# Seven PSUM banks as one ring of score tiles in a fused four-layer graph network

## The chip, the cores and the metric

The kernel runs on one core of a Trainium2 chip. The time is the device time of one execution in microseconds (us), given as the median of several runs. A separate execution is recorded by the hardware profiler; its own time stands beside its span below. TensorE, ScalarE, VectorE, GpSimd and SyncE appear as PE, ACT, DVE, POOL and SP, as in the profile; PEld is PE's weight load.

## The reference, cut to what matters

Four residual layers work on x (3327 x 128) with one dense matrix adj (3327 x 3327). Nearly all of the time goes into layer 0, an attention with 128 heads (the reference reshapes q, k and v so that the 128 features are the heads and 8 is the width of each), adj being added twice to the scores:

```python
h = jnp.maximum(_layernorm(x, axis=-1), 0.0)
q = (h @ Wq.T).reshape(d, n, 8)          # d = 128 heads, n = 3327
k = (h @ Wk.T).reshape(d, n, 8)
v = (h @ Wv.T).reshape(d, n, 8)
a = jnp.einsum('dnh,dmh->dnm', q, k) * d ** -0.5 + adj + adj
a = jax.nn.softmax(a, axis=2)
out = jnp.einsum('dnm,dmh->dnh', a, v).reshape(n, 8 * d)
x = x + out @ Wo.T
```

Three more layers follow, each built of layer norms, 128 x 128 projections and one or two products with adj. The change does not touch them.

## The kernel before, in words

**Stages.** First q, k and v are projected, split and written to DRAM, together with a bound for each row's scores (0 to about 457 us of the span). Then comes the attention (457 to 10552 us). The other three layers take the rest. Only the attention's loop is changed.

**Tiling.** Scores are held transposed: 128 keys on the partitions, up to 476 queries (a column, c, of 7; the last has 472) along the free axis. Heads go four at a time (a group, g, of 32), and the 26 key tiles two at a time (q, of 13). One (c, g, q) is a *pair* u: an even and an odd key tile of the same four heads. There are 7 x 32 x 13 = 2912 pairs. A pair needs two PSUM banks, one for each tile, of 2 KB per partition.

**What happens to a pair.** `seed` (L632, DVE) copies adj minus the row bound into the two banks. For head j = 0 `scores` (L638, PE) adds q times k onto the seed, one matmul for each tile, even (r = 0) first; the two use the upper and the lower 64 rows of the array. `exps` (L650, ACT) reads both banks in one instruction (128 x 952) and writes exp to an SBUF tile `e`. For j = 1 to 3 PE adds, onto the same banks, the next head's product together with the negated product of the last head, so that the bank again holds the scores of one head, and ACT takes the next exp. After the fourth exp (j = 3) the banks are free. `values` (L658, PE) multiplies the four `e` tiles by v, the four heads side by side in four column groups of the array, into one further bank `po`; each call is eight matmuls on PE. After 13 pairs `po` holds a group's result, and `store` (L670, DVE) copies it to `OS`, from which POOL issues four DMAs (L674). The next group's first `values` must wait for that copy, since there is one `po`.

**The order of the work** is written out by hand as a loop over slots i, one exp in each; each engine follows it in order. Slot 4m is the first exp (j = 0) of pair m, slot 4m+1 the last (j = 3) of pair m-2, slot 4m+2 the third (j = 2) of pair m-1, slot 4m+3 the second (j = 1) of pair m. So a pair's exps stand at slots 4m, 4m+3, 4m+6 and 4m+9. In every odd slot PE gets a *block*: the scores for the next two slots, then one `values` call. In slot 4m+1 that is the scores of slots 4m+2 and 4m+3 and `values` of pair m-3's odd tile; in slot 4m+3 the scores of slots 4m+4 (pair m+1, j = 0) and 4m+5, and `values` of pair m-2's even tile. The store of pair m-3, if it is the last of its group, stands in slot 4m+2. Now and then slot 4m+3 has other DVE work (`Square`: transposes and a reduction of adj, L283 and L287, about 1 us each).

**The banks before.** Seven banks are for scores, in three PSUM tiles of 3, 2 and 2 banks; pair u uses tile u % 3. With the 3-bank tile, pairs alternate between banks (0, 1) and (2, 1): the even tile's seed goes to a free bank in slot 4m, the odd tile's, in slot 4m+2, waits for the last exp of the pair three before. With a 2-bank tile both seeds stand in slot 4m+1 behind that last exp, which is issued in two halves of 128 x 476, so that the even seed can start after the first half. A one-element memset `apart` (L742) stands between the two seeds. So 1941 of the 2912 pairs have their j = 3 exp in halves.

**Dependencies.** `touch` tells the framework for each instruction that touches score banks which earlier ones it needs not wait for (other banks of the tile, on another engine; with the 2-bank tiles on DVE too), and adds a dependency on the last one that touched the same bank.

Of the kernel before, what the change touches and what calls it, by code (L numbers as in the profile page):

```python
# [9 lines left out]

DVE = mybir.EngineType.DVE
F32 = mybir.dt.float32


# [3 lines left out]
AF = mybir.ActivationFunctionType  # L18
# [5 lines left out]
P = 128  # L24
# [49 lines left out]
def width_of(c):  # L74

    return min(CW, N + 1 - c * CW)
# [8 lines left out]
def gnn_kernel(ctx: ExitStack, tc: tile.TileContext, x, adj, Wq, Wk, Wv, Wo, embed, layer,  # L85
               embed_bias, layer_bias, weight, bias, W_in, W_out, out):
    nc = tc.nc
# [171 lines left out]
    class Square:  # L259
# [29 lines left out]
        def store(self):  # L289
            nc.sync.dma_start(by_tile[:, :, self.s * P:(self.s + 1) * P].rearrange("t p n -> p t n"), self.cols)  # L290
# [144 lines left out]
    with tc.tile_pool(name="d1", bufs=1) as d1, tc.tile_pool(name="d2", bufs=2) as d2, \  # L435
# [17 lines left out]
        with tc.If(loose > 0):  # L453
            for s in range(squares_of(0), NT):
                square(d2, s, d2)
            for t in range(NT):
# [5 lines left out]
                with tc.For_i(0, HEADS, 1) as d:  # L462
# [3 lines left out]
                    for r in range(2):  # L466
                        for b in range(4):
# [4 lines left out]
                                             start=True, stop=True)  # L472
# [9 lines left out]
            for c in range(NC):  # L482
                c0 = c * CW
                w = min(CW, N - c0)
# [3 lines left out]
                with tc.For_i(0, HEADS, 1) as d:  # L488
# [11 lines left out]
                    po = d_ps.tile([P, CW], F32, name="po_x")  # L500
                    for t in range(NT):
                        m = rows_of(t)
                        s = d_ps.tile([P, 4 * P], F32, name="ps_y")
# [6 lines left out]
                                         start=(t == 0), stop=(t == NT - 1))  # L510
# [9 lines left out]
    with tc.tile_pool(name="e1", bufs=1) as e1, tc.tile_pool(name="e_adj", bufs=30) as e_adj, \  # L520
# [7 lines left out]
        VA = [e1.tile([P, NT, 4, H + 1], F32, name=f"VA{i}") for i in range(2)]  # L528

        seen = e1.tile([P, 3], F32, name="seen")  # L530
        apart = e1.tile([1, 1], F32, name="apart")
        S = [e_ps.tile([P, 3 if i == 0 else 2, 512], F32, name=f"S{i}") for i in range(3)]
        po = e_ps.tile([P, 512], F32, name="po")

        def load_qk(c, g):
# [53 lines left out]
        with tc.If(loose < 1), tc.manual_schedule():  # L589
# [4 lines left out]
            for i in range(2):  # L594
                nc.vector.memset(QS[i][:, 0, :].bitcast(F32), 0.0)

            for bank in [s[:, i, :] for s in S for i in range(s.shape[1])] + [po]:
                nc.tensor.matmul(bank[:, :CW], zero[:, :P], zero, start=True, stop=True)

            pairs = [(c, g, q) for c in range(NC) for g in range(NG) for q in range(NQ)]  # L600
            n = len(pairs)
            adj_of, shift_of, v_of, e_of, here = {}, {}, {}, {}, {}

            def banks(u):


                return [2 * (u // 3 % 2), 1] if u % 3 == 0 else [0, 1]

            touched = [deque(maxlen=12) for i in range(3)]
            last = {}
            after = mybir.DependencyInfo(mybir.DependencyClass.Sync, mybir.DependencyReason.DATA)

            def touch(u, rows, x):
                of = {banks(u)[r] for r in rows}
                for y, other in touched[u % 3]:
                    if not of & other and (x.ins.engine != y.ins.engine or u % 3 and x.ins.engine == DVE):
                        tc.declare_no_dep(x.ins, y.ins, reason="other banks")
                for i in of:  # L620
                    if (u % 3, i) in last:
                        tc.add_manual_dep(x.ins, last[u % 3, i].ins.name, after, reason="the same bank")
                    last[u % 3, i] = x
                touched[u % 3].append((x, of))

            def bank(u, r):
                return S[u % 3][:, banks(u)[r], :width_of(pairs[u][0])]

            def seed(u, r):
                c, g, q = pairs[u]  # L630
                w = width_of(c)
                touch(u, [r], nc.vector.tensor_copy(bank(u, r), adj_of[c][2 * q + r][:, :w]))  # L632

            def scores(u, j):
                c, g, q = pairs[u]
                w, b = width_of(c), (c * NG + g) % 2
                for r in range(2):
                    x = nc.tensor.matmul(  # L638
                        bank(u, r), KT[b][64 * r:64 * r + 64, max(0, j - 1), q * P:(q + 1) * P],
                        QS[b][64 * r:64 * r + 64, j, :w], start=False, stop=True, skip_group_check=True)  # L640
                    if (j, q, r) == (0, 0, 0):
                        tc.add_manual_dep(x.ins, here.pop(c * NG + g).ins.name, after, reason="the loads")
                    touch(u, [r], x)

            def exps(u, j):
                w, lo = width_of(pairs[u][0]), min(banks(u))
                e = e_of[u, j] = e_e.tile([P, 2, CW], F32, name=f"e{j}", bufs=(5, 4, 3, 2)[j])

                for a, b in ((0, 2),) if j < 3 or u % 3 == 0 else ((0, 1), (1, 2)):
                    touch(u, range(a, b), nc.scalar.activation(e[:, a:b, :w], S[u % 3][:, lo + a:lo + b, :w],  # L650
                                                               AF.Exp, scale=2.0))

            def values(u, r):
                c, g, q = pairs[u]
                w, k = width_of(c), c * NG + g
                at = banks(u)[r] - min(banks(u))
                for j in range(4):
                    nc.tensor.matmul(po[32 * j:32 * j + H + 1, :w], VA[k % 2][:, 2 * q + r, j, :],  # L658
                                     e_of[u, j][:, at, :w], start=(q == 0 and r == 0),
                                     stop=(q == NQ - 1 and r == 1))  # L660
                if r == 0:
                    return
                for j in range(4):
                    del e_of[u, j]
# [11 lines left out]
            def loads(u):  # L676

                c, g, q = pairs[u]
                k = c * NG + g
                if k + 1 < NC * NG:  # L680
                    nxt = divmod(k + 1, NG)
                    if q == 1:
                        load_qk(*nxt)
                        v_of[k + 1] = load_v(*nxt)
                    if q == 4:
                        negate_q(*nxt)
                        spread_v(*nxt, v_of.pop(k + 1))
                        here[k + 1] = all_here(*nxt)
                if c + 1 < NC and (g, q) == (0, 0):
                    plan_squares(c)  # L690
                if g == NG - 1 and c + 1 < NC:
                    if q == 0:
                        shift_of[c + 1] = load_shift(c + 1)
                        adj_of[c + 1] = []
                    while len(adj_of[c + 1]) < min(NT, 2 * q + 6):
                        adj_of[c + 1].append(load_adj(c + 1, len(adj_of[c + 1]), shift_of[c + 1]))
# [29 lines left out]
            def in_slot(i):  # L726

                j = -i % 4
                return (i - 3 * j) // 4, j


            for i in range(-4, 4 * n + 15):
                u, j = in_slot(i)
                if 0 <= u < n:
                    exps(u, j)

                u, at = (i + 4) // 4, i % 4
                if u < n and (u % 3 == 0 and at in (0, 2) or u % 3 and at == 1):
                    for r in range(2) if at == 1 else (at // 2,):
                        seed(u, r)  # L740
                        if at == 1 and r == 0:
                            nc.vector.memset(apart, 0.0)  # L742
                u = (i - 14) // 4
                if at == 2 and 0 <= u < n and pairs[u][2] == NQ - 1:
                    store(u)
                if at == 3 and i > 0:
                    for f, a in behind.pop(i // 4, ()):
                        f(*a)
                if at % 2:
                    for k in (1, 2):  # L750
                        u, j = in_slot(i + k)
                        if 0 <= u < n:
                            scores(u, j)
                    u, r = ((i - 11) // 4, 0) if at == 3 else ((i - 13) // 4, 1)
                    if 0 <= u < n:
                        values(u, r)
                if at == 0 and 0 <= i // 4 < n:
                    loads(i // 4)
# [110 lines left out]
    def arr(name, w=D):  # L869
        return big.tile([P, NT, w], F32, name=name)  # L870
# [121 lines left out]
    with tc.tile_pool(name="g1", bufs=1) as g1:  # L992
# [6 lines left out]
        a, aa = arr("a", D + 1), sm.new()  # L999
# [12 lines left out]
        f = sm.div(sm.artanh(yn, L1_MAX_TANH), yn)  # L1012
        al, be = sm.mul(al, f), sm.mul(be, f)
        y = arr("y")
# [31 lines left out]
    with tc.tile_pool(name="h1", bufs=1) as h1:  # L1046
# [4 lines left out]
        a, aa = arr("a", D + 1), sm.new()  # L1051
# [9 lines left out]
        f = sm.mul(sm.div(sm.artanh(pn, L2_MAX_TANH), pn), pf)  # L1061
        al, be = sm.mul(al, f), sm.mul(be, f)
        y = arr("y")
# [6 lines left out]
        u, rr = arr("y"), sm.new()  # L1070
# [88 lines left out]
```

## Time and profile before

| what | value |
|---|---|
| median of 3 runs | 11516.81 us (11514.25 to 11517.72) |
| the profiled execution's own time | 11513.99 us |
| its span | 11512.2 us |
| mean granted PE clock over the span; in 457 to 10552 us | 0.978; 1.00 |
| stage 457 to 10552 us | 10095 us |
| exps, L650 | 13589 instructions |
| seeds, L632 | 5824 instructions, mean 660 ns |
| scores, L638 | 23296 matmuls |
| values, L658 | 46592 matmuls |
| copies of `po`, L670 | 224 instructions, 653 ns |
| `apart`, L742 | 1941 instructions, 59 ns |

A line of the costliest groups reads: source line, engine, operation, output<-input, shapes, count | busy time in us, mean ns of one | idle time of the engine before them and who ended it. The duration of one instruction starts when it is issued to its engine; where the one before is still running, the two overlap, so that a mean duration can be longer than the step from one to the next. A line of the timeline reads: start in us, length in us, engine, line, operation and count (neighbours of a kind are merged), and in brackets the engine's idle time before it and who ended it.

### The profile page before, as it was taken

To read this page: it belongs to the slowest core of one execution; us is meant where nothing else is said; L and a number is where in the kernel's file an instruction comes from. 1 tells how busy PE (TensorE), PEld (TensorE's weight loads), DVE (VectorE), ACT (ScalarE), POOL (GpSimd) and SP (SyncE) were. 2 spreads that over 40 slices of the span, in tenths; PEclk is the share of its full clock that TensorE was granted. 3 is DMA by queue.
4 is the path that set the end of the run, shared out by engine and by line. 5 is a ranking of instruction groups with operands and counts; after the bars stand their busy time and mean duration, and the time that the engine had idled before them with its cause. 6 is when DMAs were issued, how large, how long until landed. Compare 5 with 4: busy or idle time off the path is not lost.

```text
span 11512.2 us, 196520 instructions
## 1 busy us (share of the span) xinstructions
PE 11042.9 (96%) x72980; PEld 3752.1 (33%) x72980; DVE 4640.8 (40%) x9456; ACT 10396.0 (90%) x14091; POOL 1895.0 (16%) x3261
## 2 busy tenths in 40 slices
PE   4599999999999999999999999999999999998879
PEld 2233333333333333333333333333333333333544
DVE  5344443444434343343443444434443333334633
ACT  3599999999999999999999999999999999997220
POOL 5211112111121111211112111121111211111000
PEclk7799999999999999999999999999999999999889
DMA  8755555555455554555555545555554544444447
GB/s 248 248 88 94 90 89 109 87 92 92 87 109 89 90 93 75 108 90 90 93 88 107 92 88 93 90 106 93 87 92 80 100 83 77 84 78 111 163 173 272
DMA packets 652613, 1242.80 MB, mean 108 GB/s; under 512 B 185966, under 2 KB 527990, under 8 KB 635148
## 3 DMA queue, kind: packets, MB, share of 16 engines
q1 hardware_dynamic: 609768, 1100.61, 49.0%
q0 software_dynamic: 41888, 129.51, 3.7%
q8 instruction: 590, 9.67, 0.4%
q14 instruction: 367, 3.01, 0.1%
HBM read 1082.90 MB, written 146.60 MB: 107 GB/s over the span
## 4 chain that ended last, share of the span: by engine, by line
ACT 59%; PE 31%; issue 4%; DVE 1%; DMA 0%; POOL 0%; SPq 0%; POOLq 0%; DVEq 0%; ACTq 0%
ACT e L650 59%; PE po L658 13%; PE S L638 12%; PE pu L952 5%; PE pu L904 0%; PE ps_y L848 0%; PE pu L927 0%; DVE OS L670 0%; DVE xs L939 0%; DMA ot<-oT_d 0%; PE pu L915 0%; DVE s L955 0%; DMA KT<-kS_d 0%; PE ps_t L844 0%; DVE s L935 0%
## 5 line engine op out<-in xcount | busy, mean ns | idle before, releaser
L650 ACT ACTIVATE e<-S 128x952 f32<-128x952 f32 (+3 forms) x13589 | 10091.6, 1067 | 4.0 <-PE S L638 3.7
L632 DVE COPY S<-a 128x476 f32<-128x476 f32 (+1 forms) x5824 | 3620.0, 660 | 6100.6 <-ACT e L650 6052.3
L658 PE MATMUL po<-e,VA 128*9 128x476 f32 (+1 forms) x46592 | 5737.2, 564 | 15.7 <-DVE OS L670 4.3
L638 PE MATMUL S<-QS,KT 64*128 64x476 f32 (+1 forms) x23296 | 5147.0, 446 | 24.9 <-DVE S L632 20.2
L638 PEld LDWEIGHTS S<-QS,KT 64*128 64x128 f32 x23296 | 2530.0, 183 | 5254.9 <-ACT e L650 2390.7
L674 POOL DMA_DIRECT2D oT_d<-OS x896 | 470.8, 531 | 5563.0 <-DVE OS L670 5455.6
L658 PEld LDWEIGHTS po<-e,VA 128*9 128x9 f32 x46592 | 691.6, 88 | 1644.7 <-issue 1545.0
L559 POOL TENSOR_SCALAR QS<-QS 32x476 fp32r<-32x476 f32 (+1 forms) x1344 | 781.9, 582 | 1345.7 <-DMA QS<-qS_d 772.7
L124 ACT COPY uT<-pu 128x494 f32<-128x494 f32 (+1 forms) x12 | 6.6, 546 | 426.9 <-PE pu L952 426.9
L569 POOL COPY VA<-VR 128x832 f32<-128x832 f32 x224 | 198.3, 885 | 977.2 <-DMA VR<-v_d 767.7
L952 PE MATMUL pu<-strip,h 128*128 128x494 f32 (+2 forms) x728 | 293.8, 564 | 38.9 <-ACT h L885 38.9
L952 PE MATMUL pu<-strip,y 128*128 128x494 f32 (+2 forms) x728 | 295.1, 568 | 29.2 <-DVE y L939 18.2
L580 POOL TENSOR_TENSOR a<-a,shb 128x476 f32<-128x476 f32 (+1 forms) x182 | 213.2, 1206 | 242.6 <-DMA a<-adjT 219.7
L283 DVE STREAM_TRANSPOSE cols<-rows 128x416 f32<-128x416 f32 x208 | 199.6, 964 | 21.8 <-DMA rows<-in_adj_dram 13.8
L952 PEld LDWEIGHTS pu<-strip,h 128*128 128x128 f32 (+1 forms) x728 | 138.1, 191 | 190.8 <-issue 141.4
L952 PEld LDWEIGHTS pu<-strip,y 128*128 128x128 f32 (+1 forms) x728 | 139.4, 192 | 184.1 <-issue 153.2
L670 DVE COPY OS<-po 128x476 f32<-128x476 f32 (+1 forms) x224 | 146.2, 653 | 40.9 <-PE po L658 34.1
L124 ACT COPY hT<-pu 128x494 f32<-128x494 f32 (+1 forms) x4 | 2.2, 546 | 136.2 <-PE pu L952 136.2
L415 ACT CAST st_k<-st_q 128x1664 fp32r<-128x1664 f32 x16 | 53.7, 3377 | 75.4 <-DMA st_q<-kraw_d 57.9
L955 DVE TENSOR_REDUCE s<-strip 128x1 f32<-128x3327 f32 (+1 forms) x26 | 93.9, 3616 | 61.6 <-DMA strip<-in_adj_dram 61.6
L950 POOL DMA_DIRECT2D strip<-adjT x39 | 20.8, 532 | 589.1 <-PE pu L952 576.5
L340 PE MATMUL ps_t<-wk,hT 128*128 128x512 f32 x104 | 58.8, 700 | 60.8 <-ACT sq L362 60.8
(178 smaller groups left out, 1840.1 us busy)
## 6 DMA issues: line engine op xcount, KB each, us to landing
KT<-kS_d SPq DMA_DIRECT2D x1792, 208.0 KB
KT<-kS_d SPq DMA_DIRECT2D x1792, 104.0 KB
VR<-v_d SPq DMA_DIRECT2D x224, 416.0 KB
strip<-adjT POOLq DMA_DIRECT2D x39, 1663.5 KB, 7.1
strip<-adjT SPq DMA_DIRECT2D x36, 1663.5 KB
QS<-qS_d SPq DMA_DIRECT2D x3072, 14.9 KB
QS<-qS_d SPq DMA_DIRECT2D x1536, 29.8 KB
adjT<-cols SPq DMA_DIRECT2D x26, 1664.0 KB
```

The costliest lines, as they stand in the source:

```text
L283: nc.vector.transpose(self.cols[:, t0:t0 + NQ, 32 * j:32 * j + 32], self.rows.rearrange("p (x t) -> p t x", t=NT)[:, t0:t0 + NQ, :])
L559: nc.gpsimd.tensor_scalar(QS[b][r0:r0 + 32, j + 1, :w], QS[b][r0:r0 + 32, j, :w].bitcast(F32), -1.0, 0.0, op0=ALU.mult, op1=ALU.add)
L569: nc.gpsimd.tensor_copy(VA[(c * NG + g) % 2][:, :, :, 0:H], v.rearrange("p j (t e) -> p t j e", e=H))
L580: nc.gpsimd.tensor_tensor(a[:, :w], a[:, :w], shift[:, :w], op=ALU.subtract)
L632: touch(u, [r], nc.vector.tensor_copy(bank(u, r), adj_of[c][2 * q + r][:, :w]))
L638: x = nc.tensor.matmul(bank(u, r), KT[b][64 * r:64 * r + 64, max(0, j - 1), q * P:(q + 1) * P], QS[b][64 * r:64 * r + 64, j, :w], start=Fa ...
L650: touch(u, range(a, b), nc.scalar.activation(e[:, a:b, :w], S[u % 3][:, lo + a:lo + b, :w], AF.Exp, scale=2.0))
L658: nc.tensor.matmul(po[32 * j:32 * j + H + 1, :w], VA[k % 2][:, 2 * q + r, j, :], e_of[u, j][:, at, :w], start=(q == 0 and r == 0), stop=(q ...
L670: nc.vector.tensor_copy(o[:, :w], po[:, :w])
L674: nc.gpsimd.dma_start(oT_d[:, d * N + c * CW:d * N + c * CW + w], o[32 * j:32 * j + H + 1, :w])
L952: nc.tensor.matmul(pu[c][:, :w], y[:m, t, :], s[:m, c * AW:c * AW + w], start=(t == 0), stop=(t == NT - 1))
L955: nc.vector.tensor_reduce(deg[:m, t:t + 1], s[:m], axis=AX.X, op=ALU.add)
```

## The change

The three score tiles become one tile of seven banks, a ring. Pair u takes the banks `odd = (4 - 2u) % 7` and `even = odd + 1` (modulo 7): (even, odd) is (5, 4), (3, 2), (1, 0), (6, 5), (4, 3), (2, 1), (0, 6), and then the same again. So the even bank of pair u becomes the odd bank of pair u+3, and its odd bank the even bank of pair u+4. Both seeds stand in slot 4m+1: first the odd one of pair m+1, then the even one of pair m+2, both behind the last exp of pair m-2. Only where u % 7 is 6 do the two banks not lie side by side; there each of the four exps is issued in two halves, even first. All other exps are whole. In `e` the odd tile comes first now. `apart` is gone. `touch` keeps one list of the last 48 accesses, and no longer frees a DVE instruction from waiting for another DVE instruction.

```diff
-        S = [e_ps.tile([P, 3 if i == 0 else 2, 512], F32, name=f"S{i}") for i in range(3)]
+        S = e_ps.tile([P, 7, 512], F32, name="S")
...
             def banks(u):
-                return [2 * (u // 3 % 2), 1] if u % 3 == 0 else [0, 1]
-            touched = [deque(maxlen=12) for i in range(3)]
+                odd = (4 - 2 * u) % 7
+                return (odd + 1) % 7, odd
+            touched = deque(maxlen=48)
...
-                for y, other in touched[u % 3]:
-                    if not of & other and (x.ins.engine != y.ins.engine or u % 3 and x.ins.engine == DVE):
+                for y, other in touched:
+                    if not of & other and x.ins.engine != y.ins.engine:
                         tc.declare_no_dep(x.ins, y.ins, reason="other banks")
...
             def exps(u, j):
-                w, lo = width_of(pairs[u][0]), min(banks(u))
+                w, (even, odd) = width_of(pairs[u][0]), banks(u)
                 e = e_of[u, j] = e_e.tile([P, 2, CW], F32, name=f"e{j}", bufs=(5, 4, 3, 2)[j])
-                for a, b in ((0, 2),) if j < 3 or u % 3 == 0 else ((0, 1), (1, 2)):
-                    touch(u, range(a, b), nc.scalar.activation(e[:, a:b, :w], S[u % 3][:, lo + a:lo + b, :w],
-                                                               AF.Exp, scale=2.0))
+                if even > odd:
+                    touch(u, (0, 1), nc.scalar.activation(e[:, :, :w], S[:, odd:even + 1, :w], AF.Exp, scale=2.0))
+                    return
+                for r in range(2):
+                    touch(u, [r], nc.scalar.activation(e[:, 1 - r, :w], bank(u, r), AF.Exp, scale=2.0))
...
-                u, at = (i + 4) // 4, i % 4
-                if u < n and (u % 3 == 0 and at in (0, 2) or u % 3 and at == 1):
-                    for r in range(2) if at == 1 else (at // 2,):
-                        seed(u, r)
-                        if at == 1 and r == 0:
-                            nc.vector.memset(apart, 0.0)
+                at = i % 4
+                if i == -4:
+                    seed(0, 0)
+                if at == 1:
+                    for u, r in (((i + 3) // 4, 1), ((i + 7) // 4, 0)):
+                        if u < n:
+                            seed(u, r)
```

More of the change, by code (lines that the diff above doesn't have):

```diff
@@ L9 @@
 from concourse.masks import make_identity
-DVE = mybir.EngineType.DVE
 F32 = mybir.dt.float32
@@ L530, in gnn_kernel @@
         seen = e1.tile([P, 3], F32, name="seen")
-        apart = e1.tile([1, 1], F32, name="apart")
-        S = [e_ps.tile([P, 3 if i == 0 else 2, 512], F32, name=f"S{i}") for i in range(3)]
+        S = e_ps.tile([P, 7, 512], F32, name="S")
         po = e_ps.tile([P, 512], F32, name="po")
@@ L595, in gnn_kernel @@
                 nc.vector.memset(QS[i][:, 0, :].bitcast(F32), 0.0)
-            for bank in [s[:, i, :] for s in S for i in range(s.shape[1])] + [po]:
+            for bank in [S[:, i, :] for i in range(7)] + [po]:
                 nc.tensor.matmul(bank[:, :CW], zero[:, :P], zero, start=True, stop=True)
@@ L616, in touch @@
                 of = {banks(u)[r] for r in rows}
-                for y, other in touched[u % 3]:
-                    if not of & other and (x.ins.engine != y.ins.engine or u % 3 and x.ins.engine == DVE):
+                for y, other in touched:
+                    if not of & other and x.ins.engine != y.ins.engine:
                         tc.declare_no_dep(x.ins, y.ins, reason="other banks")
                 for i in of:
[L621 to L624, printed above, removed]
+                    if i in last:
+                        tc.add_manual_dep(x.ins, last[i].ins.name, after, reason="the same bank")
+                    last[i] = x
+                touched.append((x, of))
             def bank(u, r):
-                return S[u % 3][:, banks(u)[r], :width_of(pairs[u][0])]
+                return S[:, banks(u)[r], :width_of(pairs[u][0])]
             def seed(u, r):
@@ L655, in values @@
                 w, k = width_of(c), c * NG + g
-                at = banks(u)[r] - min(banks(u))
                 for j in range(4):
                     nc.tensor.matmul(po[32 * j:32 * j + H + 1, :w], VA[k % 2][:, 2 * q + r, j, :],
-                                     e_of[u, j][:, at, :w], start=(q == 0 and r == 0),
+                                     e_of[u, j][:, 1 - r, :w], start=(q == 0 and r == 0),
                                      stop=(q == NQ - 1 and r == 1))
```

## The prediction, written before the changed kernel ran

> **What bounds the kernel now.** I read the page's busy times first, then the costliest groups, then the stage's busy time.
>
> ```profile
> PE 11042.9 (96%) x72980; PEld 3752.1 (33%) x72980; DVE 4640.8 (40%) x9456; ACT 10396.0 (90%) x14091; POOL 1895.0 (16%) x3261
> ...
> L650 ACT ACTIVATE e<-S 128x952 f32<-128x952 f32 (+3 forms) x13589 | 10091.6, 1067 | 4.0 <-PE S L638 3.7
> L632 DVE COPY S<-a 128x476 f32<-128x476 f32 (+1 forms) x5824 | 3620.0, 660 | 6100.6 <-ACT e L650 6052.3
> ```
>
> PE looks fuller than ACT, but its waits hide in modelled durations. The exps are the clearer sign: 10091.6 us busy of the 10095 us that the stage lasts, and only 4.0 us idle before all 13589 of them. So the attention is as long as ACT's exps, provided none really starts late. A busy share can't show that, since an exp counts as busy from its issue. I looked at single exps in the timeline, the first of the stage alone and then neighbours:
>
> ```profile
> 456.77 0.96 ACT L650 ACTIVATE e<-S 128x952 f32<-128x952 f32 x1
> ...
> 5003.63 2.04 ACT L650 ACTIVATE e<-S 128x952 f32<-128x952 f32 x2
> 5004.47 2.05 ACT L650 ACTIVATE e<-S 128x952 f32<-128x952 f32 x2
> 5005.32 1.67 ACT L650 ACTIVATE e<-S 128x952 f32<-128x952 f32 x2
> 5006.16 1.28 ACT L650 ACTIVATE e<-S 128x476 f32<-128x476 f32 x2
> 5006.61 1.69 ACT L650 ACTIVATE e<-S 128x476 f32<-128x476 f32 x2
> ```
>
> Start plus length is the end of the second instruction of each line: 5005.67, 5006.52, 5006.99, 5007.44, 5008.30. Whole exps end 0.86 us apart, halves 0.46. I took these steps for the whole stage: 0.857 in the mean for whole ones, 0.460 for halves, hardly any longer. An exp with nothing ahead of it takes 0.96, and the usual one 1.18 because it is issued early. So ACT never waits, with some 0.2 us to spare.
>
> **What the Trainium skill says.** "ScalarE: Activation LUTs", section "What ACT_TABLE_LOAD costs": an ACTIVATE with immediate operands takes 186 ns plus 0.833 ns per element, and neighbours overlap by about 93 ns, so each costs 93 ns beyond its elements. The trace agrees on the lone one (979 against 963 ns), less on the 93: the stage's exps have 4 x (2496 x 952 + 416 x 944) = 11,075,584 elements, 9229.7 us at 0.833; the rest of 10091.6 is 861.9 us, 63 ns each. The ends say the same (2 x 460 - 857 = 63). I use 63. "PSUM — Partial Sum Buffer", section "PSUM bank collisions raise a hardware error", has engines run clean at once in different banks; the trace has DVE seeding, PE adding and ACT reading together with ACT never held up, so I give the ring's new neighbours no cost. "VectorE: DVE Perf Modes", section "The DRAIN you can't avoid", has a semaphore between two DVE instructions cost nothing; the trace differs a little (below).
>
> **Part 1: fewer halves.** Before, 1941 exps are halved (13589 - 4 x 2912). After, one pair in seven has four halved exps: 416 x 4 = 1664, so 13312 instructions. 277 fewer at 63 ns are **17.5 us** off the path.
>
> **Part 2: the seeds, pair by pair.** Let E be the end of the exp in slot 4m+1 (j = 3 of pair m-2).
>
> ```profile
> 5003.99 0.66 DVE L632 COPY S<-a 128x476 f32<-128x476 f32 x1 [2.08 <-ACT e L650]
> 5004.50 0.55 PEld L638 LDWEIGHTS S<-QS,KT 64*128 64x128 f32 x4 [0.80 <-issue]
> ...
> 5007.02 1.25 DVE L632 COPY S<-a 128x476 f32<-128x476 f32 x2 [2.37 <-ACT e L650]
> ...
> 5007.90 0.18 PEld L638 LDWEIGHTS S<-QS,KT 64*128 64x128 f32 x1 [0.80 <-DVE apart L742]
> ...
> 5008.33 0.29 PEld L638 LDWEIGHTS S<-QS,KT 64*128 64x128 f32 x3 [0.24 <-DVE S L632]
> ```
>
> The first two lines are a pair on the 3-bank tile: even seeded long ago, one seed behind a whole exp. That is what all pairs get after. The odd seed ends at E + 0.69 (0.03 to start, 0.66), its weights load 0.05 later, its matmul takes 0.48, ACT can start 0.04 later: E + 1.26. This exp is the third after E; it would end at E + 3 x 0.857 = 2.57, so it must start by 2.57 - 0.96 = 1.61. It has 0.35 to spare; with the halves of the other lines it had less, the odd seed ending 1.28 after the first half, E + 0.82. So nothing new is exposed; and nothing is gained either, as ACT did not wait. PE works 2 x (0.63 + 0.92) = 3.1 us per pair when unhindered, ACT about 3.46. `apart` (59 ns) was off the path; its removal is worth nothing. A `Square` step (about 1 us) in slot 4m+3 starts behind the seeds, E + 1.4, and ends by E + 2.4, while the next odd seed is due at E + 3.43: hidden by a microsecond.
>
> **Part 3: the even seed ahead of the store.** Behind the even seed on DVE stands, once in 13 pairs, the copy of `po`, and PE's next `values` waits for it. Before:
>
> ```profile
> 5020.91 1.25 DVE L632 COPY S<-a 128x476 f32<-128x476 f32 x2 [2.23 <-ACT e L650]
> ...
> 5022.31 0.65 DVE L670 COPY OS<-po 128x476 f32<-128x476 f32 x1
> ...
> 5023.01 0.12 PEld L658 LDWEIGHTS po<-e,VA 128*9 128x9 f32 x8 [0.50 <-DVE OS L670]
> ...
> 5023.93 0.30 PEld L638 LDWEIGHTS S<-QS,KT 64*128 64x128 f32 x4 [0.80 <-ACT e L650]
> ```
>
> And of those who waited for `OS` in the whole run (us, times):
>
> ```profile
>   PEld po L658: 99.7, 223
> ```
>
> Here E is 5021.34, the second half's end. The seeds started half an exp earlier, the copy ended at E + 1.62, PE began at E + 1.67 and its next scores at E + 2.59. PE waits at nearly every store, 99.7 us in all, and ACT loses nothing. After, both seeds wait for the whole exp. Does the second wait for the first as well? The 3-bank tile's odd seeds do (DVE's queue has waits on DVE itself about as often as there are such pairs, 971), and the change drops the exemption, so yes. A dependent DVE step starts 0.03 after the one before (L303 to L304: 3120.84 to 3120.87). So: first seed to E + 0.69, second 0.72 to 1.38, copy 0.59 more as neighbours without a wait overlap (two seeds in 1.25), 1.97; PE 0.05 later, 2.02; its eight matmuls 0.92, 2.94; scores 0.49, 3.43; ACT could start at 3.46. That exp is slot 4m+6, the fifth after E; it must start by 5 x 0.857 - 0.96 = 3.32. **0.14 us late**, which nothing hides: ACT is never idle elsewhere. Where one of the pairs around is a halved one, it's less: none with halves at E itself (the first seed starts earlier), 0.13 less, 0.07 less and 0.06 less in three other positions. 13 and 7 share no factor, so all seven come equally often: (3 x 0.14 + 0.01 + 0.07 + 0.08) / 7 = 0.083 us, times 224 stores, **18.6 us**. Bounds: without the self-wait the second seed ends at 1.28 and 0.04 is left, near 0; with a copy that can't overlap (0.65 + 0.03) 0.23, and up to 0.34 if PE arrives late as well. PE then catches up: the next block has its scores 0.17 early.
>
> **Sum.** -17.5 + 18.6 = +1.1. On the profiled execution's 11514.0 that is 11515.1. The median of the runs is 2.8 above it: **11518 us**. The stages before and after are untouched.
>
> **The rivals.** *B, the store stays hidden:* the copy ends 0.1 us earlier than I sum; for it, PE's wait before cost ACT nothing, and the spare of an exp is some 0.2; against it, the chain above. Then only part 1 is left: 11499. *C, slower:* PE comes out of the store 0.2 us later than I sum, because copy and seed don't overlap and PE is still behind from the new group's waits on loads. A plain store then costs 0.34, the mean (6 x 0.34 - 0.26) / 7 = 0.254, 57 us in all: 11556. From 0.26 at a plain store it passes +0.2%. *D, the ring doesn't free the banks:* with one tile, the odd score also waits for the even seed. Its exp could start at E + 1.38 + 0.58 = 1.96 instead of 1.61: 0.35 in six pairs of seven, 870 us, 12390. The declared exemptions speak against it. *F, faster:* an instruction costs the skill's 93 ns and stores are free: -26, 11491.
>
> **Numbers.** A change within 0.2% (23 us) can't be told from none. Chances: my forecast (a plain store 0.05 to 0.25, 11501 to 11539) 0.50, B 0.20, C 0.23, D 0.03, F 0.04. So faster 0.04, same 0.70, slower 0.26. The range leaves out F, D and the upper part of C: 11497 to 11552.
>
> **What would show it.** 13312 exps and a mean step of whole exps still at 0.857; PE's wait for the copy of `po` growing from 99.7 to some 200 us; ACT's ends stretched by about 0.14 at the third exp of the third pair of a group and nowhere else. Wrong if whole exps step wider at every pair, or if ACT shows no late exp at stores.

## The result, and the profile after

The changed kernel takes 11525.74 us (median of 12 runs, 11522.56 to 11528.01) against 11515.68 us for the kernel before (12 runs, 11513.39 to 11519.21): 10.1 us more. The ratio is 1.0008, with a 95% interval of 0.9999 to 1.0017; the interval holds 1, but the runs of the two kernels don't overlap, and a second comparison below gives 10.5 us. The forecast was 11518 us and "same". Line numbers in the changed kernel are one or two lower than before: seeds are L631, scores L637, whole exps L648, halves L651, values L657, the copy of `po` L669.

The page of the changed kernel, its busy times and costliest groups:

```profile
PE 10947.3 (95%) x72980; PEld 3798.5 (33%) x72980; DVE 4840.5 (42%) x7515; ACT 10396.6 (90%) x13814; POOL 1895.1 (16%) x3261
...
L648 ACT ACTIVATE e<-S 128x952 f32<-128x952 f32 (+1 forms) x9984 | 9224.2, 1246 | 11.5 <-PE S L637 4.2
L631 DVE COPY S<-a 128x476 f32<-128x476 f32 (+1 forms) x5824 | 3821.3, 656 | 5940.8 <-ACT e L648 4937.8
L657 PE MATMUL po<-e,VA 128*9 128x476 f32 (+1 forms) x46592 | 5737.1, 564 | 124.9 <-DVE OS L669 124.2
...
L651 ACT ACTIVATE e<-S 128x476 f32<-128x476 f32 (+1 forms) x3328 | 2179.6, 857 | 0.6 <-PE S L637 0.3
```

There are 9984 + 3328 = 13312 exps, 277 fewer. The mean length of a whole exp of 952 columns has grown from 1181 to 1248 ns. That looks like a loss and is the contrary: an exp's length counts from its issue, so a longer one was ready earlier. What has appeared is in the line of the values: PE stood idle 124.2 us for the copy of `po`, where the page of before has 4.3, and its weight loads waited longer too.

```profile
L658 PE MATMUL po<-e,VA 128*9 128x476 f32 (+1 forms) x46592 | 5737.2, 564 | 15.7 <-DVE OS L670 4.3
```

Of those who waited for `OS` in the changed kernel (us, times; before, the first of these was 99.7):

```profile
  PEld po L657: 198.5, 222
  PE po L657: 124.2, 221
```

Those waits alone don't show that ACT lost anything. For that I took the step from the end of each exp to the end of the next. The median is 857 ns for whole ones and 460 for halves, in both kernels (850 and some 457 in the last column, which is narrower). Whatever is well above it is a late exp. I call the sum of all differences from these medians the *excess*; steps a little below their median count against it, so that its parts come to slightly more than the whole:

| from the first exp's start to the last one's end | before | changed |
|---|---|---|
| length | 10095.6 us | 10104.3 us |
| exps | 13589 | 13312 |
| excess | 2.3 us | 28.9 us |
| of that, at the third exp (j = 2) of a group's third pair, behind a store | none late | 27.8 us, 192 exps |
| of that, other exps late by more than 0.02 us | 5.3 us, 14 exps | 3.9 us, 6 exps |

The six others of the changed kernel stand in the first five pairs of the stage and in its last one. One of them, 1.08 us, is at the same exp of the very first group, which has no store ahead of it; the kernel before has it too, with 1.02. Apart from these ends, the changed kernel waits at one place only, behind 192 of the 223 stores that a group follows. One of them in the timeline:

```profile
5117.84 1.42 DVE L631 COPY S<-a 128x476 f32<-128x476 f32 x2 [2.02 <-ACT e L648]
...
5118.51 0.39 PEld L637 LDWEIGHTS S<-QS,KT 64*128 64x128 f32 x4 [0.80 <-DVE S L631]
...
5119.16 0.64 DVE L669 COPY OS<-po 128x476 f32<-128x476 f32 x1
5119.86 0.12 PEld L657 LDWEIGHTS po<-e,VA 128*9 128x9 f32 x8 [0.96 <-DVE OS L669]
5119.86 0.98 PE L657 MATMUL po<-e,VA 128*9 128x476 f32 x8 [0.62 <-DVE OS L669]
...
5120.77 0.30 PEld L637 LDWEIGHTS S<-QS,KT 64*128 64x128 f32 x4 [0.80 <-ACT e L648]
```

The two seeds take 1.42 us instead of the 1.25 of before, the copy follows straight on, and PE gets to the new group's values only at 5119.86: its weight loads have then been idle for 0.96 us, since those of the scores, and its matmuls for 0.62. The exp that the last line names had ended at 5119.52, more than a microsecond earlier; the line stands where it does because the values were late. The exps around it, by ACT's timeline alone (each line has two exps, and the second of the first line is the first of the second):

```profile
5119.20 2.02 ACT L648 ACTIVATE e<-S 128x952 f32<-128x952 f32 x2
...
5120.04 2.23 ACT L648 ACTIVATE e<-S 128x952 f32<-128x952 f32 x2
```

The first line ends at 5121.22, the second at 5122.27: a step of 1.05 in place of 0.86. That last exp started at 5121.31 and took 0.96, as one with nothing ahead of it does.

### The profile page after: what moved, and what is told of

Its sections match the earlier page's. It is cut to its first block, busy times and chain, and to the rows that moved or that the text cites. A ratio compares the mean times of both kernels' runs of the same rounds, so it can differ in the third digit from the quotient of the medians.

```text
span 11524.7 us, 200628 instructions
## 1 busy us (share of the span) xinstructions
PE 10947.3 (95%) x72980; PEld 3798.5 (33%) x72980; DVE 4840.5 (42%) x7515; ACT 10396.6 (90%) x13814; POOL 1895.1 (16%) x3261
## 4 chain that ended last, share of the span: by engine, by line
ACT 50%; PE 34%; issue 8%; DVE 3%; DMA 0%; DVEq 0%; POOL 0%; SPq 0%; POOLq 0%; ACTq 0%
ACT e L648 42%; PE po L657 15%; PE S L637 13%; ACT e L651 9%; PE pu L951 5%; DVE OS L669 1%; DVE S L631 1%; PE ps_y L847 0%; PE pu L903 0%; DMA ot<-oT_d 0%; DVE xs L938 0%; PE pu L926 0%; PE pu L914 0%; PE ps_t L843 0%; DVE s L954 0%
## 5 line engine op out<-in xcount | busy, mean ns | idle before, releaser
L648 ACT ACTIVATE e<-S 128x952 f32<-128x952 f32 (+1 forms) x9984 | 9224.2, 1246 | 11.5 <-PE S L637 4.2
L631 DVE COPY S<-a 128x476 f32<-128x476 f32 (+1 forms) x5824 | 3821.3, 656 | 5940.8 <-ACT e L648 4937.8
L657 PE MATMUL po<-e,VA 128*9 128x476 f32 (+1 forms) x46592 | 5737.1, 564 | 124.9 <-DVE OS L669 124.2
L637 PE MATMUL S<-QS,KT 64*128 64x476 f32 (+1 forms) x23296 | 5042.8, 458 | 24.1 <-DMA a<-adjT 20.0
L637 PEld LDWEIGHTS S<-QS,KT 64*128 64x128 f32 x23296 | 2569.1, 183 | 5259.4 <-ACT e L648 2053.4
L651 ACT ACTIVATE e<-S 128x476 f32<-128x476 f32 (+1 forms) x3328 | 2179.6, 857 | 0.6 <-PE S L637 0.3
L657 PEld LDWEIGHTS po<-e,VA 128*9 128x9 f32 x46592 | 694.6, 89 | 1607.2 <-issue 1407.8
L669 DVE COPY OS<-po 128x476 f32<-128x476 f32 (+1 forms) x224 | 144.2, 644 | 10.5 <-PE po L657 10.4
```

Source lines behind the costliest of these rows:

```text
L637: x = nc.tensor.matmul(bank(u, r), KT[b][64 * r:64 * r + 64, max(0, j - 1), q * P:(q + 1) * P], QS[b][64 * r:64 * r + 64, j, :w], start=Fa ...
L648: touch(u, (0, 1), nc.scalar.activation(e[:, :, :w], S[:, odd:even + 1, :w], AF.Exp, scale=2.0))
L651: touch(u, [r], nc.scalar.activation(e[:, 1 - r, :w], bank(u, r), AF.Exp, scale=2.0))
L669: nc.vector.tensor_copy(o[:, :w], po[:, :w])
```

## The experiments

Each time is compared with the kernel before on the same chip (11511.43 us beside the first four, 11510.76 beside the last three). Where an interval holds 1, the runs of the two kernels still don't overlap. Lateness is the step from end to end above its median, taken from the trace of each run.

**The copy between the seeds.** The ring as it is; the even seed goes behind the store.

```diff
-                if at == 1:
-                    for u, r in (((i + 3) // 4, 1), ((i + 7) // 4, 0)):
-                        if u < n:
-                            seed(u, r)
+                if at == 1 and (i + 3) // 4 < n:
+                    seed((i + 3) // 4, 1)
                 u = (i - 14) // 4
                 if at == 2 and 0 <= u < n and pairs[u][2] == NQ - 1:
                     store(u)
+                if i == -3:
+                    seed(1, 0)
+                if at == 2 and i > 0 and (i + 6) // 4 < n:
+                    seed((i + 6) // 4, 0)
```

> The ring kept, but on VectorE the even seed of pair m+2 stands behind the copy of po instead of ahead of it (odd seed, copy, even seed). Theory (the loss is the store waiting behind the even seed): the copy ends near E + 1.4 instead of E + 2.0, PE's next values start near E + 1.5, the scores are 0.3 us early, the late exps at stores are gone, and only the 277 exps fewer remain: 11515.7 - 17.5 = 11498, with a spread of 3. Rival (the ring itself delays PE, through one shared tile or the waits at a new group): the time stays at 11525 and the exp of slot 4m+6 is still late. If an ACTIVATE's fixed cost were 93 ns, 11490.

Measured: 11492.92 us (21 runs), ratio 0.9984 (0.9977 to 0.9990), 18.5 us below the kernel before. The excess falls from 28.9 to 0.7 us, and no exp behind a store is late. The same store as above:

```profile
5099.51 0.66 DVE L631 COPY S<-a 128x476 f32<-128x476 f32 x1 [2.01 <-ACT e L648]
...
5100.18 0.39 PEld L637 LDWEIGHTS S<-QS,KT 64*128 64x128 f32 x4 [0.80 <-DVE S L631]
...
5100.32 0.65 DVE L669 COPY OS<-po 128x476 f32<-128x476 f32 x1 [0.15 <-PE po L657]
...
5100.89 0.65 DVE L631 COPY S<-a 128x476 f32<-128x476 f32 x1
5101.03 0.12 PEld L657 LDWEIGHTS po<-e,VA 128*9 128x9 f32 x8 [0.46 <-DVE OS L669]
```

The copy now waits only for PE's last values (0.15 us), and PE begins 1.52 us after the odd seed's start, where it was 2.02 above. The theory holds, and the rival (that the ring itself delays PE) falls: the ring is unchanged here. What is left is part 1 of the forecast.

**Half an exp earlier at stores.** The order on VectorE as in the changed kernel; the exp that releases the seeds ahead of a store is halved.

```diff
-                if even > odd:
+                if even > odd and not (j == 3 and u % NQ == 0):
```

> The ring and the order on VectorE kept, but the one exp whose end releases the seeds ahead of a store (j = 3 of each group's first pair, 192 exps more than are halved already) is issued in two halves. Theory: the odd seed starts half an exp (0.46 us) earlier, the even one right behind the whole, the copy of po ends near E + 1.54, no exp is late at stores; 192 more instructions cost 192 x 63 ns = 12 us, and 28.8 us of late exps go: 11525.7 - 28.8 + 12.1 = 11509. Rival (PE is late at a new group for another reason): only the 12 us are added, 11538.

Measured: 11504.5 us (13 runs), ratio 0.9994 (0.9986 to 1.0003), 6.9 us below the kernel before, where 6.7 was expected. The excess is 0.5 us. So the same wait goes away by an earlier start of the chain too, at the price of 192 instructions: the stage is 11.8 us longer than with the copy between the seeds, 62 ns for each.

**A longer store.** 

```diff
+        filler = e1.tile([P, 200], F32, name="filler")
...
                 o = e2.tile([P, CW], F32, name="OS", bufs=1)
+                nc.vector.memset(filler, 0.0)
                 nc.vector.tensor_copy(o[:, :w], po[:, :w])
```

> The changed kernel with one more VectorE instruction, a memset of 128 x 200 that nobody uses, right ahead of each copy of po. It takes some 0.2 us there. Theory: at all stores but those where the exp at E is halved, ACT loses what the copy is later, one for one: 192 x 0.2 = 38 us more, 11564 (the profile gives the memset's own length, and the sum goes with it). Rival (the copy isn't what PE waits for last, or PE has time in hand): unchanged, 11526.

Measured: 11561.65 us (4 runs), ratio 1.0043 (1.0027 to 1.0058), 50.2 us above the kernel before and so 40.2 above the changed one. The memset's group and the whole exps' in this run:

```profile
L649 ACT ACTIVATE e<-S 128x952 f32<-128x952 f32 x8560 | 7897.9, 1231 | 37.8 <-PE S L638 37.8
...
L670 DVE MEMSET filler<- 128x200 f32 x224 | 50.4, 225 | 7.2
```

It took 0.225 us; the copy of `po` ended 0.21 later (E + 2.21 in place of 2.00), and the late exp at a plain store grew from 0.18 to 0.39 us: one for one with the copy's end. Where the exp ahead of the seeds is halved, the median exp was not late, as in the changed kernel. ACT is now idle even by the page's count (37.8 us for the exps of 952 columns, 9.9 in the changed kernel), which has only the time in which no exp is on record as running.

**The even seed first.**

```diff
-                    for u, r in (((i + 3) // 4, 1), ((i + 7) // 4, 0)):
+                    for u, r in (((i + 7) // 4, 0), ((i + 3) // 4, 1)):
```

> The two seeds in the other order: the even one of pair m+2 first, the odd one of pair m+1 behind it. Theory: an odd seed has 0.35 us in hand before its exp is late. It now ends 0.76 us later, at E + 1.45, its scores can start the exp at E + 2.02 where 1.61 is needed: 0.41 us late in every pair, 2912 x 0.4 = 1165 us, some 12690. Rival (PE, not the seed, sets when the first exp of a pair can start, so that the order doesn't matter): 11526.

Measured: 12446.12 us (one run), 934.7 above the kernel before. The first exp of a plain pair is late by a median of 0.41 us, as expected, which confirms the 0.35 us in hand. The total was expected 1165 and is 925 above the changed kernel, because I counted 0.4 for all pairs: the pairs next to a halved one are late by only 0.16 to 0.35, and a halved pair's first exp not at all. The first exps come to some 830 us of the excess of 953. Another 78 are at a place that I had not counted, the third exp of the pair ahead of each halved one (median 0.18 us).

**The kernel before, all exps whole.**

```diff
-                for a, b in ((0, 2),) if j < 3 or u % 3 == 0 else ((0, 1), (1, 2)):
+                for a, b in ((0, 2),):
```

> The kernel before with every exp whole: only the halves of the j = 3 exps on the 2-bank tiles are gone, both seeds still stand behind that exp, and none is a pair ahead. Theory (it is the seed a pair ahead, not the ring as such, that makes whole exps possible): the odd seed now ends at E + 1.28, its pair's first exp can start at E + 1.85 where 1.61 is needed, 0.24 us late in 1941 pairs, 466 us; 1941 instructions fewer save 1941 x 63 ns = 122 us: 344 us slower than the kernel before, some 11857. Rival (the spare of the exps covers the later seeds, the halves were not needed): 122 us faster, 11391.

Measured: 11895.03 us (2 runs), ratio 1.0333 (1.0312 to 1.0354), 384 us slower than the kernel before. The first exp of each pair on a 2-bank tile is late by a median of 0.25 us (0.24 expected); the excess is 509 us. Fewer instructions save 1941 x 63 ns = 122 us, and the kernel before had 2 us of excess: 509 - 2 - 122 = 385. Expected were 344: the first exps come to 488 us where I had 466, and 21 us lie at other exps. The page of this run shows the same from the other side, whole exps 985 ns long, so hardly ever ready ahead:

```profile
L650 ACT ACTIVATE e<-S 128x952 f32<-128x952 f32 x9984 | 8742.3, 985 | 249.3 <-PE S L638 66.2
```

So in this loop, with both seeds behind the exp that frees their banks, the halves saved more than they cost, and it is the seed a pair ahead that makes whole exps pay.

**The price of a half.** The version with the copy between the seeds, with 416 exps more in halves (the edit is against that version).

```diff
-                if even > odd:
+                if even > odd and not (j == 1 and u % 7 == 3):
```

> The version with the store between the seeds, with the second exp (j = 1) of one further pair in seven in halves: 416 instructions more and nothing else. At 63 ns each 26 us more than that version, 8 above the kernel before; at the skill's 93 ns 39 us more, 20 above. Rival (a half hides in the spare of the exps): no difference, 18 below the kernel before.

Measured: 11519.85 us (12 runs), ratio 1.0008 (0.9999 to 1.0017), 9.1 above the kernel before (8 expected). By the stage's length, 10102.98 against 10076.09 us, less 0.7 more of excess, it is 26.1 us, 63 ns for each. So 93 ns are out here, and nothing hides a half.

**The changed kernel again.**

> The changed kernel once more, beside the others on one chip. Theory: 10 us above the kernel before, 28 above the version with the store between the seeds. Rival (the 10 us were a matter of that chip): within 3 us of the kernel before.

Measured: 11521.29 us (12 runs), ratio 1.0008 (0.9999 to 1.0017), 10.5 above the kernel before, with an excess of 28.0 us. The 10 us are no matter of one chip.

**Not run.** One exp that reads banks 6 and 0 with a step between them would end the last 3328 halves, 1664 instructions fewer. At 63 ns each that would be 105 us, an estimate that no run here tests.

## Why the prediction was right, point by point

- **What bounds the kernel** held. The step of whole exps is 857 ns in both kernels. The count of exps and the change in excess come to +9.1 us (-17.5 + 28.9 - 2.3), and the attention is 8.7 us longer in the changed kernel's trace than in that of before.
- **Part 1** held, 17.5 us: with the stalls gone the copy-between version is 18.5 below, of which 1.6 are excess that the kernel before had (2.3 against 0.7); that leaves 16.9. The 63 ns from the trace were right against the 93 of the Trainium skill's "ScalarE: Activation LUTs", section "What ACT_TABLE_LOAD costs": by that page's figure part 1 would be an estimated 277 x 93 ns = 25.8 us.
- **Part 2** held. Apart from the two ends of the stage, no pair but those behind stores has a late exp, and the reversed seeds showed the 0.35 us in hand. Dropping `apart` was not tested alone.
- **Part 3** was right in its place and its mechanism; its size was off. Forecast 18.6 us, measured 27.8 behind stores. PE's weight loads waited 198.5 us for the copy, where some 200 were forecast. The positions among seven tell what was missing (medians): a plain store (three positions) is 0.18 us late where I summed 0.14; next to halved pairs 0.05, 0.11 and 0.12 where I had 0.01, 0.07 and 0.08; with the halves at the releasing exp none, as forecast. So one term of about 0.04 us was missing from the chain, six times in seven. Measured from E at a plain store, medians, beside my sum:

| | my sum | measured |
|---|---|---|
| odd seed ends | 0.69 | 0.69 |
| even seed starts | 0.72 | 0.79 |
| even seed ends | 1.38 | 1.45 |
| copy ends | 1.97 | 2.00 |
| PE starts the values | 2.02 | 2.05 |
| PE's next scores begin | 2.94 | 2.97 |
| ACT starts the late exp | 3.46 | 3.50 |

  The mis-sized term is the even seed's wait for the odd one: 0.10 us, not the 0.03 that I took from L303 and L304. There the waiting instruction holds the wait itself. Here it stands in an instruction of its own on DVE's queue: in the median it begins 0.04 us after the odd seed's end and takes 0.02, and the even seed starts 0.04 after that. For the seeds' line the queue has 5802 such instructions where it had 1090 (before, then changed):

```profile
L632 DVEq EVENT_SEMAPHORE  x1090: 21/21/3936, 426.1 to 10538.2; - x182
L631 DVEq EVENT_SEMAPHORE  x5802: 21/21/3929, 434.7 to 10553.1; - x194
```

  Another line, in the last stages, shows both. L182 of the changed kernel (L183 before) runs the same operation on tiles of one shape several times in a row; from the end of one to the start of the next it is 34 to 35 ns in 13 cases where the second one holds the wait, and 103 to 105 in the 4 where an instruction of its own does. In those 4 the second one also waits for ACT, which had finished at least 0.4 us before. The profile of before has the same two groups, so the 0.10 could have been read there.

  The copy gave 0.04 back: it ends 0.55 after the seed, not 0.59. The medians make 26.1 us; the other 1.7 are longer waits behind single stores (up to 0.52 us), whose cause stays open.
- **The sum.** Forecast +1.1, measured +10.1 and, in the second comparison, +10.5. The 9 us between are nearly all part 3's. Of the measured difference, 9.1 are accounted for by the terms above. The last one or two are not: the attention begins anywhere from 452.9 to 459.3 us in the nine profiles, though the work ahead of it is the same. The median lies inside the forecast's own 11501 to 11539, but that range is wide enough to hide an error of half of part 3, and B's 11499 would have been "same" as well. What tests the forecast is the late exps and their place.
- **Rivals.** B (stores hidden) and F (93 ns) are out by the late exps and by the price of a half; C's place was right, and the longer store shows its slope (0.39 us at a plain store, 68 us behind all stores; C's rule gives 67), but the changed kernel did not reach it; D is out, as no ordinary pair is late.

## What to carry to other kernels

When one engine is full, find out how late each of its inputs may come before it stalls, and add up the chain to each, not only to the one that an edit is about: here the ring eased the wait of every pair and stretched a rare one that nothing covered. Where work is done ahead of need, look at what stands behind it in the same queue, and put it last there if it can wait: here, moving the early seed behind the store's copy turned +10 us into -18.5 against the kernel before, with the same instructions.

## What the runs showed of the hardware that was not expected

- After a late exp ACT regains its lead slowly. In the median whole exps start 0.844 us apart and end 0.857 us apart, so the lead grows by only some 13 ns for each. In the changed kernel a plain exp is 963 ns long at the store, 970 at the next pair's start, and back above 1250 only five pairs later. Whether two delays closer than that add up, no run here shows.
- A dependency on the DVE instruction just before cost 0.03 us where the second instruction held the wait and 0.10 us where the wait stood in the queue as an instruction of its own, for the seeds and for L182 alike.
